# A four-layer graph network on one core: the seam between the second and the third layer is rearranged

## The chip, the cores and the metric

The kernel runs on one core of one Trainium2 chip. The metric is the device time of one execution in microseconds (us), the median of several runs. PE is the matmul engine, PEld its weight loads, DVE the vector engine, ACT the scalar engine, POOL the third compute engine, and SP issues most of the transfers (DMAs). Every engine works through its own instructions in the order of the program.

## The reference, cut to what matters

`x` is 4096 x 128 in float32, `adj` a symmetric 4096 x 4096 matrix of zeros and ones with ones on the diagonal. Four graph layers follow each other, each with a residual and a layer norm:

```python
x = _layernorm(x + _L0_gnn_ref(x, adj, ...))   # hyperbolic attention with distances
x = _layernorm(x + _L1_gnn_ref(x, adj, ...))   # attention of four heads, below
x = _layernorm(x + _L2_gnn_ref(x, adj, L2_gnn_weight))          # convolution, below
x = _layernorm(x + _L3_gnn_ref(x, adj, L3_gnn_W, ...))          # attention with leaky relu

# second layer: q, k, v of x, then per head
e     = where(adj == 0, 0, exp(q @ k.T / sqrt(32) - max))
alpha = e / sum(e)
out   = alpha @ v
beta  = sigmoid(concat([out, x_r, out - x_r]) @ Wb)      # x_r = x @ Ws + bs
y     = beta * x_r + (1 - beta) * out

# third layer
adj_hat    = adj + eye(n)
d_inv_sqrt = (sum(adj_hat, axis=1) + 1e-08) ** (-0.5)
out = relu((d_inv_sqrt[:, None] * adj_hat * d_inv_sqrt[None, :]) @ x @ weight)
```

## The kernel before, in words

The matrix is cut into 8 x 8 square tiles of 512 x 512 (`NS = 8`, `S = 512`, `NT = 32` row blocks of 128). A tile lies on the chip as `[128, 4, 512]`: in float32 1 MB, or 8 KB of each of the 128 partitions. In what follows "row 0" is the first row of eight tiles of a layer. The comments and names in the code count the layers from one or from nought; this text says first to fourth layer.

The class `Fast` runs all four layers on the shortest way, which needs some assumptions on the data (that `adj` holds only zeros and ones, that sums lie in a range). Each is looked at on the way; the findings go into columns of a tile `odd`, one column by each call of `mark()`, and at the end into two flags `good`. If a flag is 0, everything is computed again by `Net`.

**Second layer** (`layer1`, then `attention_unshifted`). KT and QT hold keys and queries, each split in two halves of float32r for an exact product; VA holds the values. The loop goes over rows I of tiles and row blocks jb (32 in a row, 256 in all). For each, `scores` makes sixteen matmuls (L2049), ACT two exponentials (L2057), DVE one masking by the adjacency tile (L2059, on 128x2048), and `sums` eight matmuls (L2076). Scores run two steps ahead of the sums. Beside this
- `copy` writes each tile of `adj` to `adjf` in the order in which the later layers read it (L2009, on SP's queue);
- `row`, `degree` and `look` read the rows of `adj` as `nat`, in halves of 128x2048, through ACT's queue (L2023). ACT sums them for the degrees (L2029), and of the row blocks 2 and 3 of each row of tiles DVE looks for values that are neither 0 nor 1, in two pieces of 128x1024 (L2038);
- `ending(I)` normalises row I. It is a generator, advanced by one item with each step of the next row. Its items hold the copy out of PSUM (L2089), transposes (L2099), products (L2106), sums (L2117), the gate (L2123 to L2129), the new X with its statistics (L2133, L2134, L211, L212), the layer norm (L2150) and Y = X times the degree factor (L2159). For the last row no row follows: what is left of the ending runs by itself, and after it a check of the softmax sums (L2200 to L2209, with a transpose on PE).

**Third layer and row 0 of the fourth** (`layers23`). One loop over 72 groups g: groups 0 to 63 are the tiles of the third layer, 64 to 71 the first row of the fourth. Tiles come from `adjf` into a ring of 8 slots; `load(g + 7)` is issued on SP's queue in group g. `halve(J)` splits Y of four row blocks into two float32r parts (ACT L2383, DVE L2384), two before the loop and then one in each group. `convolve` makes eight matmuls of 128x512 for a tile (L2403), in row 0 also eight small ones with the identity (L2395). `look` checks half of each tile on DVE (L2367, on 128x1024); the other half is what the second layer looked at. On the diagonal DVE adds the identity to a tile (L2378). `finish(I)` is a generator again and is advanced beside row I + 1: copy out of PSUM (L2435), matmul with the weights (L2439), relu (L2442), statistics, layer norm, and what the fourth layer needs of the row. `weights` and `weights_last` prepare the fourth layer's weights (L2332 to L2355), in groups 2 and 4. `attend_first` is the first row of the fourth layer (L2418, L2421); the others are in `attend_factored` (L1585, L1588).

The order of instructions on each engine is the order of the program here (`manual_schedule`). Memory is given out in pools, as a stack from the left or from the right. What a pool gives back is given out again, and the first writer of the new tile waits for the last reader of each old tile in its place (`waits = "tile"`).

Of the kernel before, what the change touches and what calls it, by code (L numbers as in the profile page):

```python
# [63 lines left out]
class Net:  # L64
# [1226 lines left out]
    def layers23(self, w2, weight, bias, a_s, a_r, out, Y):  # L1291
# [6 lines left out]
        with ExitStack() as ctx:  # L1298
# [243 lines left out]
            with tc.If(plain > 0) as cmp:  # L1542
                self.attend_factored(F, XB, rho, col, wx, tot, eps, a0, ring, out)
# [3 lines left out]
    def attend_factored(self, F, XB, rho, col, wx, tot, eps, a0, ring, out):  # L1547
        nc, tc, N, NT, NS, D, X = self.nc, self.tc, self.N, self.NT, self.NS, self.D, self.X
        with ExitStack() as ctx:
            rot = ctx.enter_context(self.pool(name="rot3", bufs=2))  # L1550
            RING = ring.shape[1]
# [22 lines left out]
            for I in range(1, NS):  # L1574
                pa = ps_a.tile([P, S], F32, tag="pa", name="pa")
                nc.tensor.matmul(pa, lhsT=tot, rhs=eps, start=True, stop=False, skip_group_check=True)
                for J in range(NS):
                    g = NS * I + J
                    if g >= NS + RING - 1:
                        nc.sync.dma_start(out=ring[:, g % RING, :, :], in_=self.whole(I, J))  # L1580
                    at = ring[:, g % RING, :, :]
# [77 lines left out]
class Fast(Net):  # L1659

    MARKS = 160
# [6 lines left out]
    def __init__(self, ctx, tc, x, adj, good):  # L1668
        super().__init__(ctx, tc, x, adj)
        self.good, self.marks = good, 0  # L1670
        self.nc.gpsimd.memset(self.odd, 0.0)

# [315 lines left out]
    def attention_unshifted(self, VA, KT, QT, at0, R, wb):  # L1988
# [4 lines left out]
        with ExitStack() as ctx:  # L1993
            rot = ctx.enter_context(self.pool(name="rotf", bufs=1))
# [30 lines left out]
            def degree():  # L2025
                n = st["row"]
                i, k = halves[n]
                nat = st["nat"]
                nc.scalar.activation(nat, nat, AF.Identity, accum_out=self.deg2[:, k, i : i + 1])  # L2029
                row(n + 1)  # L2030
                if i % 4 > 1:
                    st["look"] = [nat[:, b * N // 4 : (b + 1) * N // 4] for b in range(2)]

# [8 lines left out]
            def scores(I, jb):  # L2042
                e = ep.tile([P, NH, S], F32, tag="e", name="e")
                ps = [ps_s.tile([P, 2, S], F32, tag="s", name="ps") for _ in range(2)]
                for k in range(2):
                    for q in range(2):
                        for h in range(NH):
# [4 lines left out]
                                rhs=QT[r, q, I * S : (I + 1) * S],  # L2052
# [32 lines left out]
            def ending(I):  # L2085

                ev = rot.tile([P, 2, S], F32, tag="ev", name="ev")
# [77 lines left out]
            with tc.manual_schedule():  # L2165
# [30 lines left out]
                for _ in rest:  # L2196
                    pass
                fine = rot.tile([P, 4 * NT + 1], F32, tag="fine", name="fine")
                den = dens.rearrange("p i a g b -> p (i a g b)")
                nc.vector.tensor_scalar(fine[:, 0 : 4 * NT], den, LOW, None, op0=ALU.is_ge)  # L2200
                nc.vector.scalar_tensor_tensor(
                    fine[:, 0 : 4 * NT], den, HIGH, fine[:, 0 : 4 * NT], op0=ALU.is_le, op1=ALU.mult,
                    accum_out=fine[:, 4 * NT :],
                )
                nc.vector.tensor_scalar(fine[:, 4 * NT :], fine[:, 4 * NT :], 4.0 * NT, None, op0=ALU.not_equal)
                p = ps_s.tile([P, 2, S], F32, tag="s", name="pfine")
                nc.tensor.transpose(p[0:1, 0, 0:P], fine[:, 4 * NT :], self.ident)
                nc.vector.tensor_reduce(fine[0:1, 0:1], p[0:1, 0, 0:P], AX.X, ALU.max)
                nc.vector.tensor_scalar(self.good[:, 0:1], fine[0:1, 0:1], 0.5, None, op0=ALU.is_lt)  # L2209

    def layer1(self, Wq, bq, Wk, bk, Wv, bv, Ws, bs, Wb, R):
# [6 lines left out]
        with ExitStack() as ctx:  # L2218
            self.on_scalar = 4
            keep = ctx.enter_context(self.pool(name="keep1", bufs=1))  # L2220
            KT = keep.tile([P, 2, N], F32R, tag="KT", name="KT")
            QT = keep.tile([P, 2, N], F32R, tag="QT", name="QT")
# [15 lines left out]
            with ExitStack() as pctx:  # L2238
# [11 lines left out]
                for c in range(NC):  # L2250
                    s = slice(c * S, (c + 1) * S)
                    for T, w, bias in ((KT, wk, bkc), (QT, wq, bqc)):
                        p = self.ps_t.tile([P, S], F32, tag="pt", name="pqk")
                        nc.tensor.matmul(p, lhsT=w, rhs=XT[:, s], start=True, stop=True)
                        nc.scalar.activation(T[:, 0, s], p, AF.Identity, bias=bias)
                        nc.vector.scalar_tensor_tensor(
                            T[:, 1, s], p, bias, T[:, 0, s].bitcast(F32), op0=ALU.add, op1=ALU.subtract
# [21 lines left out]
    def layers23(self, w2, weight, bias, a_s, a_r, out, Y):  # L2279
# [6 lines left out]
        with ExitStack() as ctx:  # L2286
            RING = 8
            ring = ctx.enter_context(self.pool(name="ring", bufs=1)).tile([P, RING, 4, S], F32R, tag="ring", name="ring")
            ring32 = ring.bitcast(F32)
            halved = ctx.enter_context(self.pool(name="halved", bufs=1))  # L2290
            halves = [halved.tile([P, NT, D], F32R, tag=f"Y{k}", name=f"Y{k}") for k in range(2)]
# [64 lines left out]

            def load(g):
                nc.sync.dma_start(out=ring32[:, g % RING, :, :], in_=self.adjf[g // NS % NS, g % NS])
# [4 lines left out]
            def look(I, J):  # L2363

                at = ring32[:, (NS * I + J) % RING, 0:2, :]
# [5 lines left out]
            def diagonal(I):  # L2371


                at = ring[:, (NS * I + I) % RING, :, :]
# [5 lines left out]
            def halve(J):  # L2380

                s = slice(4 * J, 4 * J + 4)
                nc.scalar.copy(halves[0][:, s, :], Y[:, s, :])  # L2383
                nc.vector.tensor_tensor(  # L2384
                    halves[1][:, s, :], Y[:, s, :], halves[0][:, s, :].bitcast(F32), ALU.subtract
                )

            def convolve(I, J):
# [3 lines left out]
                if I == J == 0:  # L2392
                    for b in range(4):
                        for k in range(2):
                            nc.tensor.matmul(  # L2395
                                st["pa"][:, b * P : (b + 1) * P], lhsT=halves[k][:, b, :], rhs=identr,
                                start=(b == k == 0), stop=False, skip_group_check=True,
                            )
                at = ring[:, (NS * I + J) % RING, :, :]
                for jb in range(4):  # L2400
                    j = 4 * J + jb
                    for k in range(2):
                        nc.tensor.matmul(  # L2403
                            st["pa"], lhsT=halves[k][:, j, :], rhs=at[:, jb, :], start=(I > 0 and j == k == 0),
                            stop=(j == NT - 1 and k == 1), skip_group_check=True,
                        )
                if J != I or I == 0:
                    look(I, J)

            def attend_first(J):  # L2410
# [3 lines left out]
                at = ring32[:, (NS * NS + J) % RING, :, :]  # L2414
# [97 lines left out]
            with tc.manual_schedule():  # L2512
# [5 lines left out]
                for g in range(groups):  # L2518
                    I, J = g // NS, g % NS
                    if g + 2 < NS:  # L2520
                        halve(g + 2)
                    if 0 < (g + 1) // NS == (g + 1) % NS < NS:
# [6 lines left out]
                    if g == 2:  # L2529
                        weights()  # L2530
                    if g == 4:
# [13 lines left out]
            self.attend_factored(F, XB, rho, col, wx, tot, eps, a0, ring32, out)  # L2545
# [62 lines left out]
```

## Time and profile before

| | |
|---|---|
| median of 3 runs | 1984.52 us (1978.98 to 1985.79) |
| the profiled execution | 1988.08 us, span 1986.2 us, mean PE clock 0.966 |
| PE busy | 1852.3 us, 93% of the span |
| DVE busy | 1730.1 us, 87% |
| ACT busy | 1326.8 us, 67% |
| second layer, attention loop | about 754 to 1554 us, 100 us for a row of tiles |
| third layer, its tiles | about 1571 to 1726 us |

The span is the time from the first to the last instruction. PE's matmuls overlap in its pipeline, so a busy PE is not PE at its peak. The granted clock says at which share of full speed PE ran, and the DMA share is the mean busy share of the core's 16 DMA engines. "A <- B" in a line of waits says that A was released by B.

### The profile page before, as it was taken

What the parts mean: (1) busy time and instruction counts of PE and PEld (TensorE: products, weight loads), DVE (VectorE), ACT (ScalarE), POOL (GpSimd) and SP (SyncE); (2) the same over time, 40 slices, a digit from 0 to 9 for tenths busy, and PEclk for the clock granted to TensorE, in tenths of its full rate; (3) what the DMA queues carried; (4) which work ended last, traced back from release to release, by engine and by line L of the source; (5) the groups of instructions that cost most, each with busy time, mean ns of one, the idle gap of its engine ahead of it and who ended that gap; (6) DMA issues with size and microseconds to landing.
All of it is one profiled execution on the core that took longest, in us unless ns stands there. A gap on an engine that the chain in (4) does not pass through costs nothing.

```text
span 1986.2 us, 29386 instructions
## 1 busy us (share of the span) xinstructions
PE 1852.3 (93%) x11478; PEld 1011.1 (51%) x11494; DVE 1730.1 (87%) x2704; ACT 1326.8 (67%) x1679; POOL 140.6 (7%) x209
## 2 busy tenths in 40 slices
PE   6869999999998699999999999999999699999997
PEld 5347676676667364343434333434343476644443
DVE  6689999899998866899999999898989798878897
ACT  5699999999997757777777777777787322210000
POOL 2311111121100401000000000000000000000000
PEclk9889999899999999999999999999999899999999
DMA  9768989899954934666666666666667799968872
GB/s 330 163 143 147 168 137 169 152 159 157 159 128 165 345 117 143 219 216 205 211 213 209 210 208 211 210 211 208 205 214 258 263 422 421 421 249 317 302 276 87
DMA packets 159173, 434.46 MB, mean 219 GB/s; under 512 B 12092, under 2 KB 54876, under 8 KB 134448
## 3 DMA queue, kind: packets, MB, share of 16 engines
q1 hardware_dynamic: 113056, 330.74, 46.0%
q0 software_dynamic: 36608, 34.10, 15.6%
q10 hardware_dynamic: 9360, 67.64, 10.4%
q8 instruction: 92, 1.51, 0.3%
q14 instruction: 57, 0.47, 0.1%
HBM read 463.81 MB, written 102.84 MB: 285 GB/s over the span
## 4 chain that ended last, share of the span: by engine, by line
PE 49%; DVE 23%; ACT 18%; DMA 5%; issue 4%; SPq 0%; POOL 0%; ACTq 0%; DVEq 0%; POOLq 0%
PE pv L2076 13%; PE pa L1588 10%; PE ps L2049 9%; DVE e L2059 7%; ACT e L2057 4%; ACT w L1839 3%; PE pa L2403 2%; PE pi L1906 2%; PE pj L1921 2%; ACT s L1862 2%; ACT y L1858 2%; PE pz L1822 2%; DVE nat L2038 2%; DMA dj<-rows 2%; ACT y L1854 2%
## 5 line engine op out<-in xcount | busy, mean ns | idle before, releaser
L2059 DVE SCALAR_TENSOR_TENSOR e<-at,e 128x2048 f32<-128x2048 bf16 x256 | 583.6, 2287 | 80.2 <-ACT e L2057 79.3
L2057 ACT ACTIVATE e<-ps 128x1024 f32<-128x1024 f32 x512 | 496.2, 1022 | 163.6 <-PE ps L2049 156.8
L2076 PE MATMUL pv<-e,VA 128*64 128x512 f32 x2048 | 498.4, 608 | 2.8 <-DVE e L2059 2.5
L2049 PE MATMUL ps<-QT,KT 32*128 32x512 f32 x4096 | 326.4, 418 | 5.8 <-ACT e L2057 4.6
L2049 PEld LDWEIGHTS ps<-QT,KT 32*128 32x128 f32 x4096 | 187.2, 183 | 231.1 <-ACT e L2057 170.4
L2076 PEld LDWEIGHTS pv<-e,VA 128*64 128x64 f32 x2048 | 125.0, 136 | 245.6 <-issue 212.3
L1588 PE MATMUL pa<-w,Y 128*128 128x512 f32 x448 | 195.3, 594 | 0.0
L1585 DVE SCALAR_TENSOR_TENSOR w<-rho,col,ring 128x512 f32<-128x512 f32 x224 | 163.0, 746 | 24.9 <-PE pa L1588 12.3
L1822 PE MATMUL pz<-HT 128*128 128x512 f32 x288 | 158.6, 633 | 17.8 <-DVE t L1831 7.8
L1906 PE MATMUL pi<-HA,w 128*128 128x129 f32 x1152 | 158.6, 288 | 9.6 <-DVE w L1883 9.6
L1906 PEld LDWEIGHTS pi<-HA,w 128*128 128x128 f32 x1152 | 145.3, 201 | 21.6 <-issue 19.9
L2403 PE MATMUL pa<-ring,Y 128*128 128x512 f32 x512 | 131.0, 411 | 8.5 <-DVE ring L2378 7.2
L1588 PEld LDWEIGHTS pa<-w,Y 128*128 128x128 f32 x448 | 83.7, 190 | 106.2 <-issue 80.2
L2029 ACT ACTIVATE nat<-nat 128x2048 f32<-128x2048 f32 x64 | 122.6, 1915 | 2.2 <-DMA nat<-in_adj_dram 2.2
L1921 PE MATMUL pj<-HA,w 128*128 128x129 f32 x896 | 118.9, 290 | 3.7 <-DVE X L1933 1.7
L1921 PEld LDWEIGHTS pj<-HA,w 128*128 128x128 f32 x896 | 111.0, 202 | 11.7 <-issue 7.0
L2403 PEld LDWEIGHTS pa<-ring,Y 128*128 128x128 f32 x512 | 97.8, 195 | 34.8 <-DVE ring L2378 9.5
L1870 DVE SCALAR_TENSOR_TENSOR t<-t,s 128x2048 f32<-128x2048 f32 x36 | 82.3, 2286 | 24.6 <-ACT s L1862 24.6
L1831 DVE TENSOR_SCALAR t<-pz 128x512 f32<-128x512 f32 x144 | 93.2, 682 | 11.5 <-PE pz L1825 11.4
L1839 ACT ACTIVATE w<-di,dr 128x512 f32<-128x512 f32 x144 | 90.6, 707 | 0.7 <-DMA di<-rows 0.6
L1894 DVE TENSOR_TENSOR w<-w,ptz 128x512 f32<-128x512 f32 x112 | 73.4, 680 | 18.4 <-PE ptz L1889 18.1
L1879 DVE TENSOR_TENSOR t<-t,y 128x2048 f32<-128x2048 f32 x36 | 82.1, 2282 | 0.9 <-ACT t L1875 0.9
(416 smaller groups left out, 2292.3 us busy)
## 6 DMA issues: line engine op xcount, KB each, us to landing
ring<-adjf SPq DMA_DIRECT2D x128, 1024.0 KB, 10.2
adjf<-in_adj_dram SPq DMA_DIRECT2D x64, 1024.0 KB, 6.8
nat<-in_adj_dram ACTq DMA_DIRECT2D x64, 1024.0 KB, 5.1
ad<-in_adj_dram SPq DMA_DIRECT2D x36, 1024.0 KB, 8.8
adjb<-in_adj_dram POOLq DMA_DIRECT2D x64, 512.0 KB, 12.3
at<-adjb SPq DMA_DIRECT2D x63, 512.0 KB, 3.5
low<-adjb SPq DMA_DIRECT2D x28, 512.0 KB, 5.8
up<-adjb SPq DMA_DIRECT2D x20, 512.0 KB, 6.7
```

Source lines behind the costliest of these rows:

```text
L1585: nc.vector.scalar_tensor_tensor(w, rho[:, I * S : (I + 1) * S], col[:, 0, j : j + 1], at[:, jb, :], op0=ALU.max, op1=ALU.mult)
L1588: nc.tensor.matmul(pa, lhsT=F[:, j, :], rhs=w, start=False, stop=(j == NT - 1), skip_group_check=True)
L1822: nc.tensor.matmul(pz, lhsT=HT[:, j * P : (j + 1) * P], rhs=HT[:, I * S : (I + 1) * S], start=True, stop=False)
L1839: nc.scalar.activation(w[:, jb, :], st[p]["d"][k], AF.Sigmoid, bias=dr[:, 4 * J + jb : 4 * J + jb + 1])
L1906: nc.tensor.matmul(row[I, "po"][ib // 2][:, ib % 2, :], lhsT=st[p]["w0"][:, jb, ib * P : (ib + 1) * P], rhs=HA[:, 4 * J + jb, :], start=False,
L1921: nc.tensor.matmul(pj[:, a, :], lhsT=st[p]["w1"][:, ib, jb * P : (jb + 1) * P], rhs=HA[:, 4 * I + ib, :], start=(ib == 0), stop=(ib == 3),)
L2029: nc.scalar.activation(nat, nat, AF.Identity, accum_out=self.deg2[:, k, i : i + 1])
L2049: nc.tensor.matmul(ps[h // 2][:, h % 2, :], lhsT=KT[r, k, jb * P : (jb + 1) * P], rhs=QT[r, q, I * S : (I + 1) * S], start=(k == q == 0), ...
L2057: nc.scalar.activation(e[:, 2 * k : 2 * k + 2, :], ps[k], AF.Exp)
L2059: nc.vector.scalar_tensor_tensor(e, at[:, jb % 4, :].unsqueeze(1).to_broadcast([P, NH, S]), 0.0, e, op0=ALU.not_equal, op1=ALU.mult,)
L2076: nc.tensor.matmul(st["po"][h // 2][g : g + 64, :], lhsT=VA[:, o : o + 64], rhs=e[:, h, :], start=(jb == 0), stop=(jb == NT - 1), skip_gro ...
L2403: nc.tensor.matmul(st["pa"], lhsT=halves[k][:, j, :], rhs=at[:, jb, :], start=(I > 0 and j == k == 0), stop=(j == NT - 1 and k == 1), skip ...
```

## The change

Six things are changed together.

1. The last row's ending is advanced by five items after the attention loop, and the rest is handed over as `self.rest`. `layers23` advances it by six items in each group. The check of the sums becomes a function that writes to a column of `odd` instead of `good`; it is called in group 5. `good` is set to 1 at the start.
2. The tiles that the ending still needs then (`rotf`) move to the right side of the memory and are given back in group 5; `ev` gets a pool of its own.
3. The ring becomes eight tiles. Two of them (`free0`, `free1`) are taken on the right from the beginning of the second layer's attention. The other six lie where the second layer has QT and the beginning of KT. QT is cut into eight tiles, one for each row I, and placed ahead of KT, so that slots 2, 3 and 4 lie on QT of rows 0 to 5.
4. The halves of Y become eight tiles, one for each J.
5. In row 0 of the third layer `look` is left out. Instead, `degree` hands the first 512 columns of row blocks 0 and 1 of each row of tiles to the second layer's `look`: sixteen looks on 128x512.
6. `weights` moves from group 2 to group 8, `weights_last` from group 4 to group 10. The marks grow from 160 to 176 columns.

```diff
 class Fast(Net):
-    MARKS = 160
+    MARKS = 176
...
         self.nc.gpsimd.memset(self.odd, 0.0)
+        self.nc.gpsimd.memset(self.good, 1.0)
...
-            rot = ctx.enter_context(self.pool(name="rotf", bufs=1))
+            self.late, self.slots = ExitStack(), ExitStack()
+            free = self.slots.enter_context(self.pool(name="ring0", bufs=1, side="right"))
+            self.free = [free.tile([P, 4, S], F32R, tag=f"free{k}", name=f"free{k}") for k in range(2)]
+            rot = self.late.enter_context(self.pool(name="rotf", bufs=1, side="right"))
+            evp = ctx.enter_context(self.pool(name="evf", bufs=1))
...
                 if i % 4 > 1:
                     st["look"] = [nat[:, b * N // 4 : (b + 1) * N // 4] for b in range(2)]
+                elif k == 0:
+                    st["look"] = [nat[:, 0:S]]
...
-                for _ in rest:
-                    pass
-                fine = rot.tile([P, 4 * NT + 1], F32, tag="fine", name="fine")
...
-                nc.tensor.transpose(p[0:1, 0, 0:P], fine[:, 4 * NT :], self.ident)
-                nc.vector.tensor_reduce(fine[0:1, 0:1], p[0:1, 0, 0:P], AX.X, ALU.max)
-                nc.vector.tensor_scalar(self.good[:, 0:1], fine[0:1, 0:1], 0.5, None, op0=ALU.is_lt)
+                for _ in range(5):
+                    next(rest)
+                self.rest = rest
+
+                def sums_in_range():
+                    fine = rot.tile([P, 4 * NT + 1], F32, tag="fine", name="fine")
...
+                    nc.vector.tensor_scalar(self.mark(), fine[:, 4 * NT :], 4.0 * NT, None, op0=ALU.not_equal)
+
+                self.sums_in_range = sums_in_range
...
+            QT = [keep.tile([P, 2, S], F32R, tag=f"QT{I}", name=f"QT{I}") for I in range(self.NS)]
             KT = keep.tile([P, 2, N], F32R, tag="KT", name="KT")
-            QT = keep.tile([P, 2, N], F32R, tag="QT", name="QT")
...
             RING = 8
-            ring = ctx.enter_context(self.pool(name="ring", bufs=1)).tile([P, RING, 4, S], F32R, tag="ring", name="ring")
+            ctx.enter_context(self.slots)
+            ring = ctx.enter_context(self.pool(name="ring", bufs=1))
+            slots = self.free + [
+                ring.tile([P, 4, S], F32R, tag=f"ring{k}", name=f"ring{k}") for k in range(RING - len(self.free))
+            ]
...
-            halves = [halved.tile([P, NT, D], F32R, tag=f"Y{k}", name=f"Y{k}") for k in range(2)]
+            halves = [halved.tile([P, 2, 4, D], F32R, tag=f"Y{J}", name=f"Y{J}") for J in range(NS)]
...
-                if J != I or I == 0:
+                if J != I and I > 0:
                     look(I, J)
...
                     if g + 2 < NS:
                         halve(g + 2)
+                    for _ in range(6):
+                        next(self.rest, None)
+                    if g == 5:
+                        self.sums_in_range()
+                        self.late.close()
...
-                    if g == 2:
+                    if g == NS:
                         weights()
-                    if g == 4:
+                    if g == NS + 2:
                         weights_last()
```

## The prediction

> **What bounds the kernel now.** I read the page first (PE 93% busy, DVE 87%), then looked only at the seam that the change moves: the stretches around 1554 us, where the second layer's attention ends, and up to 1726 us, where the third layer's last row of tiles ends. A table by stretches (us; busy PE, PEld, DVE, ACT, POOL; granted clock, DMA share, GB/s) gives the stages:
>
> ```profile
> 1500.00:1545.00 45.00, 44.81 (x342) 17.50 (x340) 41.52 (x46) 35.27 (x41) 0.00 (x0) 0.99 0.64 224
> 1545.00:1571.00 26.00, 10.22 (x59) 4.53 (x56) 21.36 (x77) 11.74 (x21) 2.76 (x5) 0.78 0.85 327
> 1571.00:1592.00 21.00, 21.00 (x92) 17.47 (x92) 16.31 (x39) 0.94 (x2) 0.00 (x0) 0.87 0.75 275
> 1592.00:1612.00 20.00, 20.00 (x93) 15.95 (x93) 18.98 (x52) 5.96 (x20) 0.00 (x0) 1.00 1.01 422
> ...
> 1692.00:1712.00 20.00, 18.23 (x82) 13.87 (x81) 17.53 (x53) 4.81 (x16) 0.00 (x0) 1.00 1.01 421
> ...
> 1726.00:1766.00 40.00, 35.28 (x90) 15.71 (x89) 30.08 (x63) 5.18 (x17) 0.00 (x0) 0.91 0.78 312
> ```
>
> To be seen: attention fills PE; then PE does almost nothing while DVE runs the ending; row 0 of the third layer runs with a slow PE clock; from 1592 to 1726 the DMA share is 1.01 throughout. A finer cut of the same view shows the two DMA holes and the clock:
>
> ```profile
> 1540.00:1542.00 2.00, 2.00 (x22) 0.78 (x16) 2.00 (x1) 1.18 (x2) 0.00 (x0) 1.00 0.00 0
> ...
> 1560.00:1562.00 2.00, 0.00 (x0) 0.00 (x0) 1.83 (x8) 0.00 (x0) 0.00 (x0) 0.50 1.00 422
> ...
> 1572.00:1574.00 2.00, 2.00 (x6) 1.60 (x5) 2.00 (x6) 0.00 (x0) 0.00 (x0) 0.50 0.00 0
> 1574.00:1576.00 2.00, 2.00 (x6) 1.52 (x6) 1.71 (x3) 0.00 (x0) 0.00 (x0) 0.50 0.00 0
> ...
> 1578.00:1580.00 2.00, 2.00 (x13) 1.76 (x12) 0.00 (x0) 0.00 (x0) 0.00 (x0) 1.00 1.01 414
> ```
>
> The timeline tells who waits:
>
> ```profile
> 1546.96 43.09 SPq L2358 DMA_DIRECT2D ring<-adjf  x16
> ...
> 1553.72 1.41 PE L2099 MATMUL pto<-ident,ev 128*128 128x128 f32 x8
> ...
> 1569.17 1.90 DVE L2384 TENSOR_TENSOR Y<-Y,Y 128x512 fp32r<-128x512 f32 x3
> ...
> 1571.47 8.03 PE L2403 MATMUL pa<-ring,Y 128*128 128x512 f32 x24
> ...
> 1589.67 0.59 ACT L2435 COPY a<-pa 128x512 f32<-128x512 f32 x1 [18.32 <-PE pa L2403]
> ...
> 1592.09 5.72 PE L2403 MATMUL pa<-ring,Y 128*128 128x512 f32 x24
> ```
>
> The first ring load is issued at 1546.96 (the waits of the DMA queue name PE ps L2049, the last reader of the memory). Eight loads go out by 1551; the ninth leaves SP only at 1575.2, because a slot comes free when row 0's first block is consumed. PE, done with attention at about 1555, waits 14 us for the first split of Y (DVE L2384) behind the ending. So **two chains** set the end of the third layer: row 0's start (DVE), and the DMA stream, which restarts at 1575.2 and is full afterwards. One block is 1.049 MB; at 421 GB/s that is 2.49 us, 19.9 us for a row of 8. The copies out of pa (L2435) begin at 1589.7, 1607.1, 1625.4, 1644.5, 1663.2, 1686.0, 1706.4 and 1726.3: rows of 17.5 and 18.2 us while blocks are in stock, then 20.2 on average, the DMA's pace.
>
> **What the Trainium skill says.** "TensorE: Matmul & The Clock Gate", Part 1: after an idle window of about 3.4 us the array runs at half clock until a window has been busy. The trace agrees on the half: clock 0.50 from 1560 on, and back only at 1576 to 1578, 6 to 8 us after PE resumed. "DMA: Bandwidth & Descriptors", Where 436 GB/s comes from, puts the ports' ceiling at 435 GB/s and expects about 358 from HBM; here 417 to 424 is held for 130 us, so the trace stands nearer the ports. The same page, Queues, rings and completion order, says the engines go round the queues packet by packet; I use that for the last nat load below; no view here shows it directly.
>
> **The change, part by part.**
>
> 1. *Early loads.* SP issues its last copy (L2009) at 1528.4, so five ring loads can leave then: two slots are new, three lie on QT rows 0 to 5, read for the last time in attention row 5. Five blocks are 12.4 us of DMA time. From 1528 to 1540 the DMA is some 80% busy, from 1540 to 1546 not at all, so they land by about 1551, and loads 5 to 7 (released at 1547) by 1557 to 1559. Cover: PE's 44.81 of 45 us. If it is gone: the last nat load (issued 1535.1, used by ACT at 1545.6) would have half the bandwidth, 5 us instead of 2.5, and still be in time; queued behind all five blocks it would be 5 to 7 us late, and the exponentials stand behind it on ACT.
>
> 2. *Row 0 beside the ending.* PE, transposes done, needs halve(0). DVE has done two items of the ending, the o products and one pair of sums by 1557.0 (junk L2117). Then identr 0.1, halve 0.65: PE starts at 1557.7 instead of 1568.4 or 1569.9. Eight small matmuls take 1 us at full clock, a group 1.91 us (24 in 5.72). DVE then interleaves: per group one halve (0.65) and six items of the ending, which in the trace cost 3.2, 3.5, 4.0 and 0.4 us (1557.0 to 1567.4 in the timeline, less the waits). So halve(3) comes at 1562.9, halve(4) at 1567.0, halve(5) at 1571.6; from group 5 on PE is behind DVE: 1571.6 + 3 x 1.91 = 1577.3 for row 0's end, 12.4 us ahead of 1589.7. PE's holes are about 2.6 us each, shorter than the 3 to 5 us after which the clock fell before, so I count no half clock. The ACT copies of halve, the table load (1.28) and the exp of be lie under DVE's work. The check of the sums loses its transpose and PE round trip (1567.3 to 1569.1, 1.8 us), already in these times; the 0.7 us that stays comes at group 5, under PE.
>
> 3. *DMA restart.* Load 8 leaves when group 0 is done, 1560.7 instead of 1575.2: 14.5 us. Further loads follow every 1.9 us, faster than 2.49, so the stream is full at once; before, 1575 to 1590 moved 4.87 MB of 6.3 possible, 3.4 us lost, of which I give back 2.4. Supply is some 17 us ahead. The last row ends between 12.4 us (each later row keeps its time) and 17 us (arrival alone decides) earlier; as rows 3 to 7 ran at the DMA's pace, I take 15.
>
> 4. *Looks.* Out of the third layer: eight of L2367, 1.22 + 0.08 each, 10.4 us of DVE, part of it the backlog with which row 1 began. Into attention: sixteen on 128x512; L2418, same kind and size, follows at 0.68, with 0.08 of accumulator read 0.76 us, 12.2 us together. They fall after e of jb 12 and 28 (12 and 20 in the last row). In row 6 DVE idles there for 0.22 + 1.01 us (1389, 1395) and 0.75 us (1438): covered. In the last row the first has 1.19 us of idle, the second (1518) lies where DVE is the chain. I take 1 us for all, bounds 0 and 12.2.
>
> 5. *weights moved to group 8 and 10.* Eight plus two matmuls (1.2 us) and some 2.2 us of DVE copies leave row 0, where DVE waited 4.5 us for them, for row 1. Behind them on DVE stand finish(0) and the looks of row 1; row 1 grows by up to 2 us, while the DMA keeps streaming. It is inside the 15. On POOL nothing moves; their loads are issued at 1549 and not needed until group 8.
>
> 6. QT in eight tiles, evf, the memset of good, 16 more marks (the reduction L2498 took 0.31): nothing beyond 0.1 us.
>
> **Sum.** 15 less 1: 14 us. The profiled execution took 1988.1 (span 1986.2 and 1.9 around it); 1974 for it. Its time stands 3.6 above the median 1984.5; from the median, **1970.5**. After 1726 nothing changes but its place: attend_first and the fourth layer shift whole.
>
> **Rivals.** (a) *PE cold again*, or halve later than I count: if PE's holes drop the clock, groups take 3.7 us (group 0 before, 1571.5 to 1575.2) for some 7 us, row 0 ends 3 to 4 us later, supply too: gain 6 to 11, about 1976. For: two holes; against: their length. (b) *Late loads*: memory is not released as described and all loads wait for 1547. Blocks 0 to 7 land by 1567 as now; row 0 still has them in time, but load 8 starts at 1567: gain 10 to 12, about 1973. It hardly differs, so the early slots are worth little by themselves. (c) *No overlap*: a reuse wait holds halve until the ending's last reader, so only the looks, the warm-up and some copies change: gain 0 to 6, about 1981. (d) *Slower: the looks.* In attention PE and DVE alternate on the chain, DVE for some 30 us of each 100. If a look there costs not its 0.76 us but also pushes an exponential behind a 1.9 us degree on ACT, each costs up to 1.3 us: 16 x 1.3 = 21, less 15: 6 us slower, 1990.5. It decides from 15/16 = 0.94 us per look. Against: 0.75 to 1.2 us of idle follows nearly every place.
>
> **How the numbers follow.** About 0.3%, 6 us, is what a measurement here tells from no change. Forecast (12 to 18 us) 0.63, with (b) in it; (a) 0.19; more than 18, if rows 1 to 7 run at their stocked pace of 18.2 us, 0.06; (c) and partly exposed looks 0.07, within 6 us; (d) 0.05. Faster 0.87, same 0.08, slower 0.05. The range leaves out (d), most of (c) and the far end of the fast side: 1962 to 1979.
>
> **What would show it.** Right: ring loads from about 1529; the DMA not at 0 in 1540 to 1546; first L2403 near 1559 with clock 1.00; the first copy out of pa near 1577, the last near 1711; attention rows still 100 us. Wrong: attention rows of 101 us or more; the clock at 0.50 during row 0; the first split of Y still after 1565; or a last row that gains less than 10 us although row 0 gained 12, which would mean that a row is set by DVE and not by the DMA.

## The result, and the profile after

| | before | after |
|---|---|---|
| median of 20 runs each | 1983.83 us (1976.03 to 1991.11) | 1978.12 us (1971.61 to 1982.24) |
| the profiled execution | 1988.08 us, span 1986.2 | 1980.73 us, span 1978.9 |
| mean PE clock | 0.966 | 0.972 |

The ratio is 0.9972, 95% interval 0.9958 to 0.9986: 5.7 us faster, where 14 were forecast. All times here are those of undisturbed executions: one of the seven of f1 below ran at a clock of 0.832, took 2108.92 us and is left out. The two traces put the difference in two places. The copy out of PSUM that ends an attention row (`ev`, L2089 before, L2096 after) and the copy out of pa that ends a row of tiles of the third layer (L2435 before, L2448 after) serve as marks:

| us from the start of the span | before | after | gain |
|---|---|---|---|
| row 6 of attention ends | 1450.55 | 1449.92 | 0.6 |
| row 7, the last, takes | 102.4 (to 1552.98) | 110.0 (to 1559.95) | **-7.6** |
| from there to the end of row 0 | 36.7 (1589.67) | 22.9 (1582.81) | 13.8 |
| from the end of attention to that of the third layer's last row | 173.3 (1726.27) | 158.7 (1718.68) | **14.6** |
| from there to the end of the span | 259.9 | 260.2 | -0.3 |

0.6 - 7.6 + 14.6 - 0.3 = 7.3 us, the difference of the two spans. So the seam gave what was forecast, and the last attention row took half of it back.

**The seam.** The table by stretches of after, with the columns of the one shown of before (us; busy PE, PEld, DVE, ACT, POOL; granted clock, DMA share, GB/s):

```profile
1564.00:1578.00 14.00, 10.97 (x46) 8.13 (x46) 12.62 (x55) 3.66 (x11) 0.00 (x0) 1.00 0.77 287
1578.00:1584.00 6.00, 6.00 (x27) 4.90 (x27) 4.67 (x14) 0.90 (x2) 0.00 (x0) 1.00 0.87 320
1584.00:1606.00 22.00, 21.75 (x107) 17.50 (x106) 18.89 (x60) 5.96 (x20) 0.00 (x0) 1.00 1.00 411
```

And its finer cut at the two places where the DMA stood at nought before:

```profile
1540.00:1542.00 2.00, 2.00 (x22) 1.03 (x22) 2.00 (x5) 2.00 (x3) 0.00 (x0) 1.00 1.04 393
...
1564.00:1566.00 2.00, 2.00 (x11) 1.64 (x11) 1.93 (x12) 0.37 (x1) 0.00 (x0) 1.00 0.00 0
...
1572.00:1574.00 2.00, 0.76 (x3) 0.67 (x4) 1.86 (x7) 0.00 (x0) 0.00 (x0) 1.00 0.98 389
```

To be seen: the DMA moves ring blocks at 1540, while attention still runs; its second hole is shorter (some 4 us instead of 5); the clock is 1.00 all through row 0, where it had been 0.50 for the first 5 us of the work on ring tiles. The timeline of after, SP's queue and then PE, gives the starts:

```profile
712.34 0.32 SPq L2372 DMA_DIRECT2D free<-adjf  x1
...
1536.02 1.94 SPq L2372 DMA_DIRECT2D ring<-adjf  x2
...
1566.11 2.19 SPq L2372 DMA_DIRECT2D free<-adjf  x2
```
```profile
1563.17 1.00 PE L2408 MATMUL pa<-identr,Y 128*128 128x128 f32 x7 [0.87 <-DVE Y L2399]
1564.00 3.95 PE L2416 MATMUL pa<-free,Y 128*128 128x512 f32 x16
...
1573.24 1.89 PE L2416 MATMUL pa<-ring,Y 128*128 128x512 f32 x7 [1.40 <-DVE Y L2399]
1575.96 0.50 PE L2416 MATMUL pa<-ring,Y 128*128 128x512 f32 x1 [0.82 <-ACT Y L2398]
1577.26 5.51 PE L2416 MATMUL pa<-ring,Y 128*128 128x512 f32 x23 [0.80 <-DVE Y L2399]
```

Five ring loads leave early, but not together. The two on the new slots leave at 712.3 and 769.2, each some 7 us after the copy that writes its tile (705.09 and 762.66) and far ahead of the other copies, although those copies stand before the loads in the program. The other three leave from 1536.0 on, after SP's last copy. PE reaches its first ring tile 4.0 us after the end of attention (1559.95) instead of 18.5 us, and then waits three times, 3.0 us together, for halves: DVE's part of them stands among the ending's items.

What held PE in before is seen in its timeline:

```profile
1568.20 0.37 PE L2207 MATMUL pfine<-ident,fine 128*1 128x128 f32 x1 [13.07 <-DVE fine L2205]
```

PE waited 13.07 us for the check of the sums, whose transpose stood ahead of row 0, and only then 1.12 us for the first split of Y, to which the prediction puts the whole wait. Load 8 leaves 6.2 us after the end of attention (1566.11), before 22.3 us after it (1575.23).

**The last attention row.** The waits of this stretch (engine and line, who releases it: us in all, times, longest), first before from 1450 to 1555, then after from 1450 to 1560:

```profile
ACT nat L2029 <- DMA nat<-in_adj_dram: 2.2, 3, 1.9
```
```profile
ACT nat L2034 <- DMA nat<-in_adj_dram: 4.4, 3, 3.9
...
ACT e L2064 <- DVE nat L2045: 3.4, 1, 3.4
```

One wait has grown and one is new: a degree sum on ACT waits 3.9 us for its nat load (1.9 at most before), and an exponential on ACT waits 3.4 us "for DVE's look at nat", although an exponential reads no nat. The timelines tell what stands between. `nat` has two buffers. After, at the first place:

```profile
1487.56 0.68 DVE L2045 SCALAR_TENSOR_TENSOR nat<-nat 128x512 f32<-128x512 f32 x1
...
1488.33 0.33 ACTq L2028 DMA_DIRECT2D nat<-in_adj_dram  x1
...
1496.72 1.91 ACT L2034 ACTIVATE nat<-nat 128x2048 f32<-128x2048 f32 x1 [3.92 <-DMA nat<-in_adj_dram]
```

and before, at the same place:

```profile
1486.18 0.34 ACTq L2023 DMA_DIRECT2D nat<-in_adj_dram  x1
...
1493.90 1.91 ACT L2029 ACTIVATE nat<-nat 128x2048 f32<-128x2048 f32 x1 [1.86 <-DMA nat<-in_adj_dram]
```

Before, no look was made on this half (number 56 of 64), and its buffer could be loaded again as soon as ACT had summed it. Now the new look on the strip reads it; the load leaves when the look is done (0.68 + 0.08 us from 1487.56). Counted from the end of row 6 it leaves at 38.4 instead of 35.6 us, takes 8.4 instead of 7.7 us, and the sum behind it comes 3.4 us later. At the second place, after:

```profile
1515.79 0.08 DVE L2045 DVE_READ_ACCUMULATOR nat<-nat 128x1 f32 x1
1515.96 0.33 ACTq L2028 DMA_DIRECT2D nat<-in_adj_dram  x1
1516.34 1.94 ACT L2064 ACTIVATE e<-ps 128x1024 f32<-128x1024 f32 x2 [3.44 <-DVE nat L2045]
```

The load is issued by ACT, and the exponential stands behind the load on ACT. The load leaves as soon as the second look at half 59 is done. Before, it left right behind ACT's sum of half 60 (1510.13), ahead of that same look (1511.88), and the exponential waited 0.47 us. So it must have gone into the buffer of half 60 there; now half 60 has its strip still to be looked at (1523.38), and the load has to take the other buffer. The traces don't name the buffers; this is read from the times. The exponential's wait has grown by 3.0 us. The Trainium skill, "TensorE: Matmul & The Clock Gate", row "Engine queue depth" of its first table, says that ScalarE's queue is a strict FIFO; the 0.05 us between the end of the load's issue (1516.29) and the exponential agree.

What these two delays do to PE, after and then before:

```profile
1500.21 1.68 PE L2056 MATMUL ps<-QT,KT 32*128 32x512 f32 x14 [3.93 <-ACT e L2064]
...
1517.42 1.78 PE L2056 MATMUL ps<-QT,KT 32*128 32x512 f32 x14 [3.08 <-ACT e L2064]
```
```profile
1497.44 1.69 PE L2049 MATMUL ps<-QT,KT 32*128 32x512 f32 x14 [1.87 <-ACT e L2057]
```

PE stands still for 3.9 and 3.1 us where it stood for 1.9 us once, and each time its granted clock then falls to 0.50 for 3.4 us. The whole last row in one stretch each, and one of the slow stretches of after:

```profile
1450.55:1552.98 102.43, 98.83 (x744) 39.06 (x744) 92.01 (x113) 78.65 (x89) 2.76 (x5) 0.98 0.64 224
```
```profile
1449.92:1559.95 110.03, 100.09 (x743) 39.44 (x744) 93.42 (x117) 78.87 (x88) 2.48 (x5) 0.97 0.66 238
...
1502.00:1504.00 2.00, 2.00 (x6) 0.59 (x8) 1.97 (x4) 1.70 (x3) 0.00 (x0) 0.50 0.48 201
```

PE is idle for 9.9 us instead of 3.6, and busy for 100.1 instead of 98.8 with the same matmuls: 6.3 us of the loss are waits, 1.3 us are PE's lower clock after them.

Why only the last row? Sums are made at every fourth step, and the last row has two more, at jb 13 and 17, two steps behind a sum instead of four. In the other rows a look has four steps' time until its buffer is wanted.

### The profile page after: what moved, and what is told of

Same layout as the page of the kernel before. It is cut to its first block, busy times and chain, and to the rows that moved or that the text cites. A ratio compares the mean times of both kernels' runs of the same rounds, so it can differ in the third digit from the quotient of the medians.

```text
span 1978.9 us, 29419 instructions
## 1 busy us (share of the span) xinstructions
PE 1850.4 (94%) x11493; PEld 1004.6 (51%) x11493; DVE 1727.4 (87%) x2718; ACT 1327.2 (67%) x1679; POOL 140.6 (7%) x210
## 4 chain that ended last, share of the span: by engine, by line
PE 46%; DVE 25%; ACT 19%; issue 5%; DMA 5%; SPq 0%; ACTq 0%; POOL 0%; DVEq 0%; POOLq 0%
PE pv L2083 13%; PE pa L1588 10%; PE ps L2056 9%; DVE e L2066 7%; ACT e L2064 3%; ACT w L1840 3%; ACT s L1863 2%; ACT y L1859 2%; DVE t L1871 2%; DVE nat L2045 2%; ACT y L1855 2%; PE pa L2416 2%; DMA ring<-adjf 2%; DMA dj<-rows 2%; PE pz L1823 2%
## 5 line engine op out<-in xcount | busy, mean ns | idle before, releaser
L1588 PEld LDWEIGHTS pa<-w,Y 128*128 128x128 f32 x448 | 83.7, 190 | 106.1 <-issue 80.7
L1585 DVE SCALAR_TENSOR_TENSOR w<-rho,col,ring 128x512 f32<-128x512 f32 x168 | 120.9, 744 | 7.9
L1922 PEld LDWEIGHTS pj<-HA,w 128*128 128x128 f32 x896 | 110.9, 202 | 12.4 <-issue 7.1
L2416 PE MATMUL pa<-ring,Y 128*128 128x512 f32 x384 | 97.1, 402 | 11.9 <-DVE ring L2392 7.4
L2045 DVE SCALAR_TENSOR_TENSOR nat<-nat 128x1024 f32<-128x1024 f32 (+1 forms) x80 | 88.7, 1110 | 0.0
L2416 PEld LDWEIGHTS pa<-ring,Y 128*128 128x128 f32 x384 | 71.2, 189 | 33.6 <-DVE ring L2392 9.7
```

The source lines that it names most:

```text
L1588: nc.tensor.matmul(pa, lhsT=F[:, j, :], rhs=w, start=False, stop=(j == NT - 1), skip_group_check=True)
L1922: nc.tensor.matmul(pj[:, a, :], lhsT=st[p]["w1"][:, ib, jb * P : (jb + 1) * P], rhs=HA[:, 4 * I + ib, :], start=(ib == 0), stop=(ib == 3),)
L2045: nc.vector.scalar_tensor_tensor(a, a, 0.0, a, op0=ALU.not_equal, op1=ALU.not_equal, accum_out=self.mark())
L2416: nc.tensor.matmul(st["pa"], lhsT=halves[J][:, k, jb, :], rhs=at[:, jb, :], start=(I > 0 and j == k == 0), stop=(j == NT - 1 and k == 1), ...
```

## The experiments

"A" in the expectations is the theory just told: the look holds the buffer, ACT stands behind the load. Its first rival is the looks' own time on DVE, 0.76 us each. "Last row" is row 7 of attention, "stage" the time from its end to that of the third layer's last row; 110.0 and 158.7 us in after.

| kernel | time, us | ratio to before (95%) | last row | stage |
|---|---|---|---|---|
| e1, no strip looks in row 7 | 1968.25 | 0.9924 (0.9897 to 0.9950) | 101.0 | 158.0 |
| v1, no extra sums in row 7 | 1968.38 | 0.9923 (0.9906 to 0.9939) | 98.9 | 157.7 |
| e2, before with the looks moved | 1991.91 | 1.0041 (1.0021 to 1.0061) | 109.6 | 172.4 |
| v4, extra sums in rows 2 and 4 | 1979.36 | 0.9973 (0.9956 to 0.9990) | 98.9 | 155.6 |
| f1, no look on half 56 | 1974.87 | 0.9956 (0.9935 to 0.9977) | 106.1 | 156.3 |
| f2, no look on half 60 | 1976.74 | 0.9956 (0.9939 to 0.9973) | 106.7 | 158.0 |
| f3, three nat buffers | 1971.49 | 0.9938 (0.9915 to 0.9960) | 100.7 | 157.7 |
| e3, ending issued first | 1974.66 | 0.9956 (0.9941 to 0.9971) | 110.0 | 155.1 |
| e4, two early slots | 1980.34 | 0.9975 (0.9961 to 0.9989) | 109.3 | 161.1 |
| e6, row 0 waits for the ending | 1994.68 | 1.0047 (1.0029 to 1.0066) | 109.9 | 172.5 |
| v3, row 7's strip looked at in the ring | 1963.94 | 0.9903 (0.9877 to 0.9929) | 102.8 | 155.4 |
| v7, three buffers, ending first | 1967.27 | 0.9909 (0.9880 to 0.9937) | 100.7 | 156.0 |

Before ran at 1983.9 to 1984.6 us beside these.

**e1: the strip looks of the last row left out.**

```diff
-                elif k == 0:
+                elif k == 0 and i < 4 * (NS - 1):
```

> The changed kernel, but its two looks at the strip in the last row of attention (halves 56 and 60) are left out, so that part of the check is not made; all else as changed. Theory A (the looks hold the nat buffers in the one row where sums for the degrees follow each other after two steps, so nat loads leave late and ACT stands): the last row comes back from 110.0 to about 102.5 us, the time to about 1971, 7 us below the changed kernel, ratio to before 0.9935. Rival B (it is the looks' own 0.76 us on DVE): the last row shortens by at most 1.5 us, 1976.5. Rival C (the longer last row was chance): no difference, 1978.

Measured: 1968.25 us, the last row 101.0. Two looks of 0.76 us are gone and 9.0 us with them, so it isn't their time on DVE. Both waits are gone (the sum's is 0.7 us at most), and so are both stretches at half clock: the mean clock of the row is 1.00. In v3 below, whose last row has the same code, one such stretch is left (mean 0.98) and the row takes 102.8 us; single rows can differ by that much.

**v1: the looks stay, the extra sums go.** The halves that they served are summed in row 0, at jb 3 and 7.

```diff
-                        if jb % 4 == 3 and (I or jb > 8) or I == NS - 1 and jb in (13, 17):
+                        if jb % 4 == 3:
```

> The changed kernel with the sums for the degrees begun at jb 3 of row 0 of attention, one in every four steps in all rows, and no extra ones at jb 13 and 17 of the last row; everything is computed. Theory A: the last row falls to about 100 us, 10 below the changed kernel; row 0 gets two more sums and may grow by up to 2 us (its first nat load is asked for after one group of four steps): 1968 to 1970. Rival B: the looks still cost DVE 0.76 us each, the last row stays above 108: 1977. Rival C: 1978.

Measured: 1968.38 us; the last row takes 98.9 us with its strip looks in it. Rows 1 to 6, whose looks are shifted, take 100.6 us instead of 100.0. So where the next load is four steps away the looks cost next to nothing.

**e2: the looks alone**, in before. `MARKS` grows to 176 as in after.

```diff
+                elif k == 0:
+                    st["look"] = [nat[:, 0:S]]
...
-                if J != I or I == 0:
+                if J != I and I > 0:
```

> The kernel before with only the looks moved: sixteen on the strip in attention, none in row 0 of the third layer. Theory A: rows 0 to 6 of attention stay at 100 us, the last row grows by 7 to about 109.5; row 0 of the third layer loses 10.4 us of DVE but is held by its cold PE, so 1 to 3 us come back: 1988 to 1990, slower than before by about 5. Rival B: last row plus 1.5, 1983. Rival C: 1982.

Measured: 1991.91 us, slower than before. The last row is 109.6 us, with the same two waits in its list from 1452 to 1563 (in this kernel's own line numbers):

```profile
ACT nat L2029 <- DMA nat<-in_adj_dram: 4.0, 2, 3.7
ACT e L2059 <- DVE nat L2040: 3.4, 1, 3.4
```

and what the looks leave behind in row 0 shortens the stage by 0.9 us only (173.3 to 172.4). By itself this part loses.

**f1 and f2: one of the two looks at a time.** Neither strip is looked at elsewhere.

```diff
-                elif k == 0:
+                elif k == 0 and n != 56:
```

> The kernel after without the look at the strip in half 56 alone (the first of the two in the last row; that part of the strip is looked at nowhere else). Theory A with two separate stalls: the sum of half 58 comes some 3.4 us earlier in the row, the second stall stays; last row about 106.5 us, time about 1974.7. If the first stall is the cause of the second: last row 102 to 103, time about 1971. If the first costs nothing in the end: 110, 1978.

f2 has `n != 60` instead.

> The kernel after without the look at the strip in half 60 alone (the second of the two in the last row; that part of the strip is looked at nowhere else). Theory A with two separate stalls: the sum of half 58 stays late by 3.4 us, that of half 61 loses the rest of its lateness of 7.4; last row about 106 us, time about 1974. If the second stall only follows from the first: last row 109 to 110, time about 1978.

Measured: last rows of 106.1 and 106.7 us, so 3.9 and 3.3 us less. Each look has a loss of its own, 7.2 us together. In f2 the load that had waited leaves at 1518.17, ahead of the second look at half 59 (1519.91), as in before; this fits the account of the two buffers. The list of waits agrees: without the first, the 3.9 us wait of the sum is 1.5 at most and the exponential's 3.4 stays; without the second, the exponential's is gone and the sum's stays.

**f3: a third nat buffer, every look where it was.**

```diff
-            natp = ctx.enter_context(self.pool(name="natf", bufs=2))
+            natp = ctx.enter_context(self.pool(name="natf", bufs=3))
```

> The kernel after with three nat buffers instead of two; every look stays where it is. Theory A (the look holds the buffer that the next nat load needs, and ACT stands behind that load): the load no longer waits for the look, so the last attention row falls from 110.0 us to about 102.5 (that of the kernel before, 102.4, is allowed for two extra sums), the stage behind it stays at about 158.7, and the time is about 1971, 7 us less than after. Theory B (the looks cost DVE's own time in a row that DVE carries): the last row stays at 109 to 110 us and the time at 1978. In between: one load still waits, 105 to 107 us and 1974.

Measured: 1971.49 us, the last row 100.7 us. The timeline at the first of the two places:

```profile
1483.13 0.33 ACTq L2028 DMA_DIRECT2D nat<-in_adj_dram  x1
...
1486.27 0.68 DVE L2045 SCALAR_TENSOR_TENSOR nat<-nat 128x512 f32<-128x512 f32 x1
...
1489.85 1.92 ACT L2034 ACTIVATE nat<-nat 128x2048 f32<-128x2048 f32 x1
```

The load leaves 3 us ahead of the look, and the sum waits for nothing. The row is even 1.7 us shorter than before's 102.4: the wait of 1.86 us that before's sum had for its load is gone too, and with it the hole on PE and the 3.4 us at half clock behind it (mean clock 1.00 instead of 0.98). Whether a third buffer would have helped before by itself wasn't tried.

**v4: is it two extra sums in one row, or each by itself?** Made on e3: one extra sum each in rows 2 and 4, none in row 7.

```diff
-                        if jb % 4 == 3 and (I or jb > 8) or I == NS - 1 and jb in (13, 17):
+                        if jb % 4 == 3 and (I or jb > 8) or I in (2, 4) and jb == 13:
```

> Everything is computed, ending emitted first, all sixteen looks in attention, but the two extra sums for the degrees stand at jb 13 of rows 2 and 4, one in each, not both in the last row. Theory A: each extra sum stalls ACT by the wait for its nat load and the look, 1 to 4 us each, the last row falls to 99 to 100 us: 4 to 9 us below the run with the ending first, 1966 to 1971. Rival B (looks' own time): no gain, 1975.

A miss. Rows 2 and 4 took 108.5 and 106.9 us instead of 100, and rows 3, 5 and 6, whose looks are shifted by then, 100.6. The waits of row 2, from 946 to 1056:

```profile
ACT nat L2034 <- DMA nat<-in_adj_dram: 4.1, 2, 3.9
```

So a single extra sum two steps behind a half with a strip look is enough in these two rows as well. The cost is above the 1 to 4 us that were expected: beside the wait and the sum itself, the mean clock of rows 2 and 4 is 0.97, against 1.00 in row 3, which the expectation left out.

**e3: the ending issued whole, ahead of row 0.**

```diff
-                for _ in range(5):
-                    next(rest)
+                for _ in rest:
+                    pass
```

> The changed kernel, but the last row's ending is run to its end before the third layer starts (no overlap); early ring loads, split tiles, looks and weights as changed. If the overlap brings the gain by moving the start of row 0 and the restart of the transfers: the first matmul of row 0 comes 10 to 11 us later after the end of attention than in the changed kernel, with PE cold, minus what DVE then no longer does beside row 0: 8 to 10 us slower than the changed kernel, 1987. Rival (the early loads and the missing looks make the gain, the overlap little): within 3 us of the changed kernel, 1980.

A miss. Row 0 still ran beside the ending, and the stage is 3.6 us shorter than in after. Over all runs with the early loads the difference is smaller: 155.1 to 156.0 us in the four with the ending issued first, 156.3 to 158.7 in the six with the interleave written out, some 2 us. DVE's timeline:

```profile
1558.64 0.28 DVE L2124 SCALAR_TENSOR_TENSOR junk<-o,wb 128x128 f32<-128x128 f32 x1
1558.84 0.08 DVE L2124 DVE_READ_ACCUMULATOR junk<-o,wb 128x1 f32 x1
1558.84 0.69 DVE L2399 TENSOR_TENSOR Y<-Y,Y 128x512 fp32r<-128x512 f32 x1
```

Halves (L2399) stand among the ending's sums (L2124), one after each, though the code issues the whole ending first. The text ahead of the prediction says that the order on each engine is that of the program; for DVE at this seam it is not, nor for SP with the two early loads at 712 and 769 us. After its first ring tile PE waits 1.4 and 0.2 us for halves here. What places the instructions so is open. So is which of the parts that stayed (the check that no longer uses PE, the ending's tiles on the right side, the eight tiles of halves) lets row 0 start early: no run takes them apart.

**e6: row 0 made to wait for the ending.** Made on e3: the identity that PE needs first is multiplied by a 1 computed from the ending's last Y.

```diff
-            nc.vector.tensor_copy(identr, self.ident)
+            one = pre.tile([P, 1], F32, tag="one", name="one")
+            nc.vector.tensor_scalar(one, Y[:, NT - 1, D - 1 : D], 0.0, 1.0, op0=ALU.mult, op1=ALU.add)
+            nc.vector.tensor_scalar(identr, self.ident, one[:, 0:1], None, op0=ALU.mult)
```

> The run with the ending emitted first showed that the splits of Y and the ending's rest were still interleaved on DVE, and PE still began 3 us after attention. Here the same kernel, but the identity that PE needs first in row 0 is computed from the last Y of the ending, so that row 0 cannot start before the ending is done; early loads, looks and tiles as in the run before. If the overlap is the gain: PE starts some 17 us after the end of attention, cold, load 8 leaves some 14 us later, and the time is 10 to 14 us above the run with the ending first, 1985 to 1989, as slow as before or slower. Rival (early loads and the looks taken out are enough): within 4 us of 1975.

Measured: 1994.68 us, stage 172.5 against 155.1 of e3. Its waits and its table by stretches:

```profile
PE pa L2410 <- DVE identr L2323: 16.2, 1, 16.2
```
```profile
1566.00:1568.00 2.00, 0.00 (x0) 0.00 (x0) 2.00 (x10) 2.00 (x4) 0.00 (x0) 0.87 0.01 0
...
1584.00:1586.00 2.00, 2.00 (x9) 1.60 (x8) 0.00 (x0) 0.00 (x0) 0.00 (x0) 0.87 0.00 0
```

PE waits 16.2 us, falls to half clock (0.50 between these two lines), and the DMA stands at 0 from 1566 to 1586. The overlap is worth 17.4 us of the stage and 20.0 us of the time, more than the 10 to 14 expected. Without it the other parts leave 0.8 us (172.5 against 173.3 of before): early loads have no value if nobody consumes them and nothing frees the slots.

**e4: two early slots instead of five.** KT stands ahead of QT again, so that the slots in the ring's memory come free at the end of attention.

```diff
-            QT = [keep.tile([P, 2, S], F32R, tag=f"QT{I}", name=f"QT{I}") for I in range(self.NS)]
             KT = keep.tile([P, 2, N], F32R, tag="KT", name="KT")
+            QT = [keep.tile([P, 2, S], F32R, tag=f"QT{I}", name=f"QT{I}") for I in range(self.NS)]
```

> The changed kernel with KT placed ahead of QT, so slots 2 to 7 of the ring lie on KT and the first QT tiles that are read to the end: two loads leave early instead of five. By the step on early loads: six loads leave at the last scores and end about 10 us after the end of attention, where in the changed kernel the transfers had a hole of 3.5 us before load 8; so the stream is later by 2 to 4 us: 1981. Rival (the early slots are what makes the gain): the 12 us of data come back, 1988 or more. Rival (worth nothing): 1978.

Measured: stage 161.1 us. Two loads left early as in after, and six at 1556.0, 6 us before the end of attention. Row 0 takes 22.9 us as in after, and the loss is in the later rows. Three of the five slots are worth 2.4 us against after, whose stage is the longest of the six named under e3. The whole times don't tell the two apart (0.9975 and 0.9972).

**v3 and v7: what the runs point to.** Both are e3 with the loss in the last row taken away. v3 makes no strip looks in row 7 and looks at that tile in the ring instead:

```diff
-                elif k == 0:
+                elif k == 0 and i < 4 * (NS - 1):
...
-                if J != I and I > 0:
+                if J != I and (I > 0 or J == NS - 1):
```

> Everything is computed. Ending emitted first as above; the last row's strip is looked at in the ring (tile 7 of row 0, one look of 1.3 us) and not in attention. Theory A: the last row of attention at 101 to 102.5 us, the rest as with the ending first: 7 to 8 us below that run, 1966 to 1968. If the look in row 0 of the third layer stands on the chain: 1.3 us more.

v7 has f3's third buffer.

> The kernel after with three nat buffers in the second layer and with the ending issued whole ahead of row 0: the two edits that helped, put together, with every look where after has it. If they add (last attention row 110.0 to 100.7 us by the third buffer, the stage behind it 158.7 to 155.1 by the order): the last row about 101 us, the stage about 155, the time 1966 (after 1978, less 9 and 3.5); it is then level with the version that makes the last row's looks in the ring (1964). If the order's gain was only a matter of how late the last row ended: stage 157.7 as with the third buffer alone, time 1970 to 1971.

Measured: 1963.94 and 1967.27 us, ratios of 0.9903 and 0.9909 whose intervals overlap. Everything is computed in both. They beat before and after, by 17 to 20 and 11 to 14 us. In v7 the buffer's gain is whole (last row 100.7, expected 101). The stage is 156.0 us: 1.7 less than the 157.7 of f3, about half of the 3.6 that the order was expected to bring (155).

## Why the prediction was wrong, step by step

*Early loads:* right in number and use, not in time. Three left at 1536, behind SP's last copy, which the stalls in the last row had made later than in before. The two on the new slots left 824 and 767 us before these, since SP's order is not that of the program. By e4 the slots over QT are worth 2.4 us; rival (b) said that "the early slots are worth little by themselves", which holds.

*Row 0 beside the ending:* right. From the end of attention to that of row 0 the prediction's sum had 24.3 us (1577.3 less 1553.0), measured 22.9. PE's holes were 1.4, 0.8 and 0.8 us instead of some 2.6 each, and the clock stayed at 1.00. That it stayed was in part luck: of the seven kernels with the interleave written out two fell to half clock there. The prediction ruled half clock out because the holes were shorter than the 3 to 5 us after which the clock had fallen; but before's own trace has it at 0.50 behind the hole of 1.87 us in the last row, and e1, whose holes in row 0 are nearly those of after, shows

```profile
1568.73 7.11 PE L2416 MATMUL pa<-ring,Y 128*128 128x512 f32 x23 [0.80 <-DVE Y L2399]
```
```profile
1570.00:1571.00 1.00, 1.00 (x3) 0.72 (x3) 0.93 (x4) 0.00 (x0) 0.00 (x0) 0.50 1.03 434
```

where the same 23 matmuls took 5.51 us in after. In e1 and f3 row 0 takes 24.5 us for this reason, in after, f1, f2, v1 and e4 22.9. What was believed of the interleave, that writing it out is what brings the overlap, e3 shows to be wrong; it costs some 2 us.

*DMA restart:* right in sum, with errors that cancel. "I take 15": 14.6. Of this, row 0 gave 13.8 where 12.4 were counted, and the later rows 0.8 where 2.6 were. Load 8 left 6.2 us after the end of attention, forecast 7.7 (1560.7 less 1553.0).

*Looks:* **this step failed.** "I take 1 us for all, bounds 0 and 12.2." Fourteen of the sixteen cost nothing: rows 1 to 6 took 100.0 us before and after, and row 0, from its first exponential, 102.3 us in both. The two in the last row cost 7.6 us, inside the bounds but far from the 1 us taken. The term was mis-sized because it asked only whether DVE has idle time at those places. It named the last row's places (jb 12 and 20) and the idle beside them, but never asked who waits for the buffer that a look reads, although the look is a second reader of `nat`, and ACT issues the load that reuses it. f3 shows that it is the buffer: the same looks with a third one cost nothing. e1, f1 and f2 show that each of the two looks has its part, and the traces how the late ACT leaves PE idle and then at half clock.

*weights, and the rest:* the sizes fit. Row 1 took 18.9 instead of 17.5 us (17.5 in e2 too, where the weights weren't moved), within the 2 us given, and the program after the third layer moved by 0.3 us.

*The sum:* 15 - 1 was 14.6 - 7.6, and small remainders. With three buffers in place of two (f3) the time is 1971.5 us beside a before of 1984.6, so 13.1 us faster (by the interval 8 to 17): the forecast of 1970.5 was that of a kernel without this one coupling. It fits so well in part by chance, since f3 also loses a wait and the half clock behind it that before had in its last row.

*The rivals:* (a) didn't happen in after, but for 3.4 us in e1 and f3. (c) didn't happen. e6 shows what it would have been: 1994.7 us, of which some 7.4 are the last row's loss (109.9 against 102.4); without that about 1987, an estimate from these figures, and not 1981. (d) named the right engine, an exponential on ACT that is pushed back, but as sixteen times 1.3 us behind a degree sum; it was twice some 3.8 us, behind a load or what a late load delays. The text's own test, "attention rows of 101 us or more", is what was seen, in one row of eight; but that row had taken 102.4 us in before already.

## What to carry to other kernels

A new reader of a rotating buffer is priced not only by its own duration: follow the buffer to its next load, see which engine's queue issues that load, and count what stands behind it. Look at the place where the spacing of the reuses is shortest, not at the average one; a row that is filled with two extra items is such a place. One more buffer tells such a coupling from the reader's own time in a single run. A wait that reaches PE can cost more than itself: look at the granted clock behind it.

## What the runs showed beyond that

In e6, PE's last matmul ended at 1564.3 and its clock fell at about 1567.5 (0.87 as the mean of 1566 to 1568 is 1.5 us of full clock), 3.2 us later; it came back at about 1584.5, 4 us after PE had resumed at 1580.48. In the kernel before it fell 4.2 us after the last matmul and came back 6.5 us after PE had resumed at 1569.9. The Trainium skill ("TensorE: Matmul & The Clock Gate", Part 1) speaks of an idle window of about 3.4 us. The length agrees: the clock stood at 0.50 for 3.41 us at a time, or a multiple of it (17.1 us in before and in e6). That the window must be idle as a whole does not: holes of 1.4 to 1.9 us were enough.

The traces show more. The times at which the clock changed lie on a grid of 3.41 us in each trace. Take the stretches of this grid at full clock from the end of row 6 to that of row 0, in all fourteen traces, and PE's idle time in each. After less than 1.54 us of it the next stretch was never at 0.50 (497 stretches); after 1.54 us or more it was in 23 of 26. So the same holes can cost nothing or a stretch at half clock, by where they fall on the grid: in after the worst stretch of row 0 had 1.52 us, in e1 1.62.

The nat load at the first place, 1 MB, took 8.4 us from issue to the release of the sum. It left 2.5 us behind a copy of the same size on SP's queue (1485.84), and the DMA was busy nearly throughout from 1489 to 1494. In before, load and copy left 0.3 us apart, and it took 7.7 us. So a buffer that comes free 2 to 3 us late costs nearly that whole time as soon as the sum is due within 8 us.
